# A four-layer block on one core: the second attention's queries and keys brought to heads by DMA instead of by VectorE

## The chip, the core and the metric

The kernel runs on one core of one Trainium2 chip. The metric is device time in microseconds (us) of one execution. TensorE (PE) does the matmuls and the 128x128 turnings (a matmul with the identity), VectorE (DVE), ScalarE (ACT) and GpSimd (POOL) do the elementwise work, and SyncE (SP) issues nearly all DMAs. Everything is float32; the first feed-forward layer uses float32r pieces. In PSUM there are eight banks of 128x512 float32.

## The reference

Four layers follow each other on x of (8, 512, 256), each ending in `x = layernorm(x + layer(x))`: a retention layer, a feed-forward layer with ternary weights, the second attention, and a mixture of eight experts. The change is in the third, whose heart is this (H = 16 heads of HD = 16 features):

```python
xn = _rms(x, g1)
Q, K, V = (einsum('bsf,ef->bse', xn, W).reshape(b, s, H, HD) for W in (Wq, Wk, Wv))
pQ, pK = elu(Q), elu(K)
Q1, Q2 = split(pQ, 2, axis=-1);  K1, K2 = split(pK, 2, axis=-1)
kv1 = einsum('bshe,bshd->bsed', K1, V) * SCALE     # sums over the heads of one token
kv2 = einsum('bshe,bshd->bsed', K2, V) * SCALE
w1  = einsum('bshe,bsed->bshd', Q1, kv1)
w2  = einsum('bshe,bsed->bshd', Q2, kv2)
attn = w1 - lmb * w2
```

After it come two RMS norms, a two-matmul GELU layer and the residual. The attention is over the 16 heads of one token, not over tokens.

## The kernel before

**Tiling.** The kernel works on one batch element b (512 tokens, four chunks c of 128) at a time. A group of 8 tokens with 16 heads makes 128 rows, so the attention of 8 tokens is one 128x128 score matrix in which `tokmask` keeps the pairs of equal tokens. A chunk has 16 such groups. The queries and keys of a group must lie with the 16 features of a head on 16 partitions; four groups r sit on partitions 32r to 32r+15 of one tile, and their four score matmuls (16 rows each) run beside each other on PE.

**Stages.** Each batch runs through stages a0, a1, a2 (retention), b and bn (feed-forward and norm), c1 (second attention), c2 (its norms, GELU layer and residual, store to DRAM), t (choice of experts). When four batches of a group are through, r (route) and then g, d, h, e, s (gather, experts, combine) run for the group. w loads expert weights (1 MB each).

**c1 before.** `transposed` turns the 512 tokens to x2T (features on partitions) through PE and ACT. `project(c)` makes q and k of a chunk as tokens x 512 features (line 1400) and v (line 1406); ACT and DVE apply ELU with the token's RMS factor as a scale and write `pad`; two DVE stream transposes (32x32 blocks; `V.transpose`) turn `pad` into `hT`, one for q and k and one for v. `scores(c)` turns the v part back with four PE transposes to `v_tp` (line 1454), which ACT copies to `vt`, and makes the scores `hs` (16 groups, line 1460). `masked` moves scores to `hm` with the mask (three of four on DVE, one on ACT and POOL). `values(c)` multiplies `vt` with them into `at_ps` (line 1475), and one DVE stream transpose moves that to `ap`. All of it stays on the chip.

**Order.** All engines' instruction orders are fixed at build time. A planner, `interleave`, walks through the streams of stages; each op has a cost in us and is placed on its engine's time line, and each PE step waits (`need`) until its input and a PSUM bank are free by the plan. Of the steps that can go next, it takes the smallest `t + w * due`, where `due` comes from a table `turns` in the source, one number for each stage; before, w is 0.0, so `due` only breaks ties. When PE would idle over 1.4 us by the plan, it places filler matmuls (`spare`, line 337) to keep PE's clock up. SP's DMAs are placed in the order of their planned times; SP's own issue time is not in the plan. Every engine, SP included, runs its list in order, so an instruction that waits holds back all behind it.

**DMA in flight.** A DMA issued by SP waits for the eighth DMA before it (the program gives them eight semaphores in turn), so at most eight are under way.

**Buffers.** Named slots with counts, such as `ex` (3 tiles of 128x512), `T` (3), `b8` (2), and the banks of PSUM; a stage takes slots when it begins or when it needs them, and the plan's free times order the reuse.

Of the kernel before, what the change touches and what calls it, by code (L numbers as in the profile page):

```python
# [46 lines left out]
def _constants():  # L47
# [15 lines left out]
        "parity": np.stack([hp % 2 == 0, hp % 2 == 1], 1),  # L63
        "tokmask": (i[:, None] % 8 == i[None, :] % 8) * QK_SCALE,
# [17 lines left out]
def tile_layers(ctx: ExitStack, tc: tile.TileContext, ins, out, at):  # L82
# [31 lines left out]
    iota, tokid = table("iota"), table("tokid")  # L114
# [7 lines left out]
    y_d = [dram.tile([TG + P, D], F32, name=f"y_d{g}") for g in range(G)]  # L122

# [19 lines left out]
    NVZ, XH = 3, 2  # L143
    SCM = 8
    XB, TB, EX, B8 = 4, 3, 3, 2
    EW = 3

    class Plan:
# [13 lines left out]
                hT3=2, ln=2, vz=NVZ, xh=XH,  # L162
# [129 lines left out]

    def later(t):

        return "other", t

    def interleave(streams, due):
# [11 lines left out]
        first = {"a0", "a1", "b", "c1", "h", "e", "s", "d", "z"}  # L309
        while any(queues):  # L310
            best = None
            for i, q in enumerate(queues):
# [15 lines left out]
                choice = t + 0.0 * due(key), due(key), i, on_pe, t  # L328
# [58 lines left out]
    def transposed(dst, src, t, cost=0.44):  # L387

        for k in range(NK):
            yield from need(t)  # L390
            ps = bank("tp")
            for c in range(NC):
                T.transpose(ps[:, c * P : (c + 1) * P], src[:, c, k * P : (k + 1) * P], ident)
            done = op(ACT, 0.59, pe(cost), A.copy, dst[:, k, :], ps, bank=ps)
        return done
# [222 lines left out]
    with ExitStack() as stages:  # L618
# [224 lines left out]
        pad = [wts.tile([P, 3 * D + HD], F32, name=f"pad_{i}") for i in range(2)]  # L843

        def by_head(pd, i, n):

            return pd[:, i * D : (i + n) * D].rearrange("p (h d) -> p h d", d=HD)

        def blocks(pd, i, n):

            v = by_head(pd, i, n)
            (pstep, pn), (hstep, hn), (dstep, _) = v.ap
            return bass.AP(v.tensor, v.offset, [(pstep, pn), (hstep, hn), (dstep, 2 * HD)])


        def prepare_l1():
            for i in range(2):
                op(POOL, 0.1, Plan.t, GP.memset, pad[i][:, 3 * D :], 0.0)
# [32 lines left out]
            def lam():  # L891
                nc.vector.tensor_tensor(lamv, le[:, 1:2], le[:, 0:1], ALU.subtract)
                return nc.vector.tensor_scalar(lamv, lamv, LAMBDA_INIT, None, ALU.subtract)

            op(DVE, 0.3, t, lam)
# [469 lines left out]
        def stage_bn(b):  # L1365
# [5 lines left out]
            rs1 = wk.tile([P, 2, NC], F32, tag="rms1", bufs=2, name=f"rms1_{b}")  # L1371

            def squares():
                nc.vector.tensor_tensor(rs1[:, 0], rs, rs, ALU.mult)
                return nc.vector.tensor_tensor(rs1[:, 0], rs1[:, 0], mv[:, :, 1], ALU.mult)
# [3 lines left out]
            t = rsqrt(rs1[:, 0], rs1[:, 0], 1.0, RMS_EPS, t)  # L1379
            t = op(DVS, 0.17, t, V.tensor_scalar, rs1[:, 1], rs1[:, 0], -1.0, None, ALU.mult)  # L1380
# [4 lines left out]

        def stage_c1(b):
            x2, rs1, scaled = x2s[b]
            x2T = slot_tile(wk, "T", [P, NK, S], f"x2T_{b}")
            ready = yield from transposed(x2T, x2, 0.0)
            ap = slot_tile(wk, "b8", [P, NC, H, 32], f"ap_{b}")  # L1390
            hTs = {}

            def project(c):

                cs = slice(c * P, (c + 1) * P)
                pd = pad[c % 2]
                yield from need(ready, n=2)
                qk = bank("qk_ps")
                for k in range(NK):
                    T.matmul(  # L1400
                        qk, x2T[:, k, cs], l1T[:, k, 0:2, :].rearrange("p a d -> p (a d)"),
                        start=(k == 0), stop=(k == NK - 1),
                    )
                v = bank("v_ps")
                for k in range(NK):
                    T.matmul(
                        v[:, :D], x2T[:, k, cs], l1T[:, k, 2, :], start=(k == 0), stop=(k == NK - 1)
                    )
                t = pe(2.4)
                t_qk = max(t - 0.8, scaled)  # L1410
                t = max(t, scaled)

                rs, rsn = rs1[:, 0, c : c + 1], rs1[:, 1, c : c + 1]
                ex = slot_tile(wk, "ex", [P, S], "ex")
                pqk = by_head(pd, 0, 2)
                e1 = op(ACT, 0.68, t_qk, A.activation, ex, qk, AF.Relu, scale=rsn, use=ex)
                e2 = op(
                    ACT, 0.68, t_qk, A.activation,
                    pqk, qk.rearrange("p (h d) -> p h d", d=HD), AF.Relu, scale=rs,
                )  # L1420
                release(qk, max(e1, e2))
                e1 = op(EXP, 0.63, e1, A.activation, ex, ex, AF.Exp, scale=-1.0)
                ev = op(
                    ACT, 0.46, t, A.activation, by_head(pd, 2, 1),
                    v[:, :D].rearrange("p (h d) -> p h d", d=HD), AF.Copy, scale=rs, bank=v,
                )
                t = op(
                    DVS, 0.69, max(e1, e2), V.scalar_tensor_tensor, pqk,
                    ex.rearrange("p (h d) -> p h d", d=HD), -1.0, pqk, ALU.add, ALU.add, drop=ex,
                )  # L1430
                q2 = by_head(pd, 0, 1)[:, :, HD // 2 :]
                t = op(ACT, 0.35, t, A.activation, q2, q2, AF.Copy, scale=lamv)


                hT = slot_tile(wk, "hT3", [P, 4, 3 * P], f"hT_{b}_{c}")
                turned = hT.rearrange("p g (x t) -> p x g t", t=8)
                ev = op(
                    DVE, 0.7, ev, V.transpose, turned[:, 2 * H :],
                    blocks(pd, 2, 1), use=hT,
                )  # L1440
                t = op(
                    DVE, 1.22, t, V.transpose, turned[:, : 2 * H],
                    blocks(pd, 0, 2),
                )
                hTs[c] = hT
                return max(t, ev)

            def scores(c, t):

                hT = hTs[c]  # L1450
                yield from need_scores(t, 5)
                ps = bank("v_tp")
                for g in range(4):
                    T.transpose(ps[:, g * P : (g + 1) * P], hT[:, g, 2 * P :], ident)
                vt = wk.tile([P, 4, P], F32, tag="vt", bufs=2, name=f"vt_{b}_{c}")
                sc = [bank(f"hs_{b}_{c}_{r}") for r in range(4)]
                for g in range(4):
                    for r in range(4):
                        rows = slice(32 * r, 32 * r + HD)
                        T.matmul(  # L1460
                            sc[r][:, g * P : (g + 1) * P], hT[rows, g, P : 2 * P], hT[rows, g, :P],
                            start=True, stop=True,
                        )
                t = pe(1.69)
                give(hT, t)
                scm, done = masked(f"hm_{b}_{c}", sc, tokmask, t)
                e = op(ACT, 0.59, t - 1.1, A.copy, vt.rearrange("p g n -> p (g n)"), ps, bank=ps)
                return vt, scm, max(done, e)

            def values(c, vt, scm, t):  # L1470
                yield from need(t)
                acc = bank("at_ps")
                for g in range(4):
                    for r in range(4):
                        T.matmul(
                            acc[32 * r : 32 * r + 32, g * P : (g + 1) * P],
                            vt[:, g, 32 * r : 32 * r + 32], scm[r][:, g, :], start=True, stop=True,
                        )
# [8 lines left out]
            turned = []  # L1487
            for c in range(2):
                turned.append((yield from project(c)))
            for c in range(NC):  # L1490
                full = yield from scores(c, turned[c])
                if c + 2 < NC:
                    turned.append((yield from project(c + 2)))
                    if c + 2 == NC - 1:
                        give(x2T, Plan.now)
                done = yield from values(c, *full)
            aps[b] = ap, done
# [408 lines left out]
        def after(*keys):  # L1906
# [24 lines left out]
            "c2": [(("c2", b), after(("c1", b)), {"m4": 2}, stage_c2(b)) for b in range(B)],  # L1931
            "bn": [(("bn", b), after(("b", b)), {}, stage_bn(b)) for b in range(B)],
            "c1": [
                (("c1", b), after(("bn", b), ("p", 1)), {"b8": 1, "T": 1}, stage_c1(b))
                for b in range(B)
            ],
# [55 lines left out]
                -0.67, 7.77, 120.34, 10.79, 107.15, 110.57, 2.87, 102.1, -5.72, 13.07, 11.66, -10.22,  # L1992
                100.38, 2.06, 1.79, 103.04
            ],
            "p": [-7.83, -1.63],
            "a0": [
                16.46, -2.45, 101.53, 13.47, 112.66, 108.34, 4.55, 2.62, 5.58, 13.37, 7.99, 9.62, 106.9,
                15.6, 13.84, 112.95
# [69 lines left out]
```

## Time and profile before

| what | value |
|---|---|
| median of 3 runs | 912.31 us (911.98 to 914.94) |
| the profiled execution's own time | 912.14 us |
| its span, first to last instruction | 910.1 us |
| busy PE, DVE, ACT, POOL | 857.3, 644.4, 567.3, 367.1 us |
| granted PE clock, mean over the span | 0.981 |
| DMA packets | 54252, 64.97 MB |

PE "busy" is the union of matmul records whose ends are modelled, so that a matmul's record is longer than the step from its start to the next one's. Where a price of PE time is wanted, the distance of starts in the timeline is the better measure. A float32 matmul is two records. The list of waits names for each wait the thing that came last.

### The profile page before, as it was taken

What the parts mean: (1) busy time and instruction counts of PE and PEld (TensorE: products, weight loads), DVE (VectorE), ACT (ScalarE), POOL (GpSimd) and SP (SyncE); (2) the same over time, 40 slices, a digit from 0 to 9 for tenths busy, and PEclk for the clock granted to TensorE, in tenths of its full rate; (3) what the DMA queues carried; (4) which work ended last, traced back from release to release, by engine and by line L of the source; (5) the groups of instructions that cost most, each with busy time, mean ns of one, the idle gap of its engine ahead of it and who ended that gap; (6) DMA issues with size and microseconds to landing.
All of it is one profiled execution on the core that took longest, in us unless ns stands there. A gap on an engine that the chain in (4) does not pass through costs nothing. (4 is left out here: it accounts for less than half of the span.)

```text
span 910.1 us, 20170 instructions
## 1 busy us (share of the span) xinstructions
PE 857.3 (94%) x8114; PEld 712.4 (78%) x8114; DVE 644.4 (71%) x1631; ACT 567.3 (62%) x1146; POOL 367.1 (40%) x379
## 2 busy tenths in 40 slices
PE   7989999999999999999999899998899999999942
PEld 5878978878788787878878678877577989899941
DVE  3944688888888989878778897988988643514123
ACT  2447587868779776876877867687767353132212
POOL 2124454535453533445524443353354222452233
PEclk9999999999999999999999999999999999999975
DMA  6120101010010020010200004101220557278743
GB/s 198 37 88 24 36 13 36 13 36 2 13 48 13 2 81 3 12 36 2 71 1 2 1 25 165 68 1 48 93 82 25 177 162 246 37 232 273 227 119 107
DMA packets 54252, 64.97 MB, mean 71 GB/s; under 512 B 5936, under 2 KB 49136, under 8 KB 54160
## 3 DMA queue, kind: packets, MB, share of 16 engines
q1 hardware_dynamic: 50304, 58.12, 19.0%
q0 software_dynamic: 3856, 5.57, 3.1%
q8 instruction: 64, 1.05, 0.5%
q14 instruction: 28, 0.23, 0.1%
HBM read 47.95 MB, written 15.73 MB: 70 GB/s over the span
## 5 line engine op out<-in xcount | busy, mean ns | idle before, releaser
L226 POOL TENSOR_TENSOR fsq<-fsq,fh 128x256 f32<-128x256 f32 x96 | 71.2, 742 | 61.1 <-ACT fh L226 43.4
L226 DVE SCALAR_TENSOR_TENSOR fT<-fh,lnf,fT 128x256 fp32r<-128x256 f32 x128 | 71.7, 608 | 21.5 <-ACT fT L226 21.3
L1710 PE MATMUL wo_ps<-e_hT,wo 128*128 128x160 f32 x512 | 74.1, 301 | 0.0
L1683 PE MATMUL wi_ps<-xsT,wi 128*128 128x160 f32 x512 | 73.9, 300 | 0.0
L226 DVE TENSOR_TENSOR scm<-sc,cst 128x512 f32<-128x512 f32 x96 | 61.2, 682 | 16.3 <-PE sc L1060 16.2
L1275 PE MATMUL fc_ps<-x1T,fcT 128*128 128x256 f32 x512 | 69.4, 288 | 2.7 <-ACT fh L226 1.9
L1683 PEld LDWEIGHTS wi_ps<-xsT,wi 128*128 128x128 f32 x512 | 70.6, 190 | 1.3 <-issue 1.1
L1316 PE MATMUL pr_ps<-prT,fT 128*128 128x258 f32 x512 | 69.8, 290 | 1.6 <-DVE hm L226 1.3
L1710 PEld LDWEIGHTS wo_ps<-e_hT,wo 128*128 128x128 f32 x512 | 70.3, 190 | 1.2 <-issue 0.6
L226 ACT ACTIVATE e_hT<-wi_ps 128x480 f32<-128x480 f32 (+1 forms) x48 | 25.0, 525 | 73.0 <-PE wi_ps L1683 73.0
L1275 PEld LDWEIGHTS fc_ps<-x1T,fcT 128*128 128x128 f32 x512 | 63.1, 189 | 7.3 <-ACT fh L226 2.3
L1316 PEld LDWEIGHTS pr_ps<-prT,fT 128*128 128x128 f32 x512 | 64.3, 189 | 4.0 <-DVE hm L226 1.7
L991 PE MATMUL qk_ps<-xT,wqkv 128*128 128x256 f32 x256 | 63.4, 399 | 4.0 <-ACT xT L226 2.7
L226 POOL TENSOR_TENSOR scm<-scm,cst 128x512 f32<-128x512 f32 x32 | 41.4, 1294 | 60.3 <-ACT scm L226 24.7
L226 DVE STREAM_TRANSPOSE hT<-pad 128x512 f32<-128x512 f32 (+1 forms) x64 | 60.1, 962 | 6.1 <-ACT pad L226 5.6
L226 POOL DMA_INDIRECT y_d<-eo,srci x21 | 32.8, 1563 | 73.9 <-ACT eo L226 20.7
L1400 PE MATMUL qk_ps<-l1T,x2T 128*128 128x512 f32 x128 | 61.3, 601 | 0.0
L226 DVE TENSOR_TENSOR hm<-hs,cst 128x512 f32<-128x512 f32 x96 | 60.7, 678 | 0.7 <-PE hs L1460 0.7
L226 POOL TENSOR_TENSOR ln<-ln,mhalf 128x4 f32<-128x4 f32 x32 | 33.7, 1054 | 67.7 <-DVE ln L226 67.5
L991 PEld LDWEIGHTS qk_ps<-xT,wqkv 128*128 128x128 f32 x256 | 49.1, 198 | 13.4 <-ACT xT L226 5.8
L226 ACT ACTIVATE fT<-fh,lnf 128x256 fp32r<-128x256 f32 x128 | 57.8, 498 | 1.2
L226 POOL TENSOR_TENSOR hm<-hm,cst 128x512 f32<-128x512 f32 x32 | 40.9, 1279 | 42.5 <-ACT hm L226 21.2
(267 smaller groups left out, 2057.5 us busy)
## 6 DMA issues: line engine op xcount, KB each, us to landing
wi<-in_L_ffn_wi SPq DMA_DIRECT2D x13, 1024.0 KB, 7.8
wo<-in_L_ffn_wo SPq DMA_DIRECT2D x13, 1024.0 KB, 7.7
xh<-in_L_attn_x SPq DMA_DIRECT2D x16, 256.0 KB, 2.7
x<-in_L_attn_x SPq DMA_DIRECT2D x8, 512.0 KB, 4.1
x_d<-a SPq DMA_DIRECT2D x8, 512.0 KB, 2.9
y_d<-a SPq DMA_DIRECT2D x8, 512.0 KB, 4.3
z<-y_d SPq DMA_DIRECT2D x8, 512.0 KB, 6.8
out<-z SPq DMA_DIRECT2D x8, 512.0 KB, 3.2
```

Source lines behind the costliest of these rows:

```text
L226: heapq.heappush(Plan.events, (t, Plan.count, shares, t + cost, lambda: fn(*args, **kw)))
L991: T.matmul(ps[:, m * HT : (m + 1) * HT], wqkv[:, k, which * D + m * P : which * D + (m + 1) * P], xT[:, k, :], start=(k == 0), stop=(k == ...
L1275: T.matmul(ps[:, j * HT : (j + 1) * HT], fcT[:, k, f * P : (f + 1) * P], x[:, k, :], start=(k == 0 and x is low), stop=(k == NK - 1 and x ...
L1316: T.matmul(acc[:, : D + 2], hs[:, part, f, c * P : (c + 1) * P], prT[:, f, :], start=(f == 0 and part == 1), stop=(f == NF - 1 and part == 0),
L1400: T.matmul(qk, x2T[:, k, cs], l1T[:, k, 0:2, :].rearrange("p a d -> p (a d)"), start=(k == 0), stop=(k == NK - 1),)
L1683: T.matmul(ps[:, f * CAP : (f + 1) * CAP], wi[:, k, (f3 + f) * P : (f3 + f + 1) * P], x[:, k, es], start=(k == 0), stop=(k == NK - 1),)
L1710: T.matmul(ps[:, m * CAP : (m + 1) * CAP], wo[:, f, m * P : (m + 1) * P], hT[:, f, :], start=(f == 0), stop=(f == NF - 1),)
```

## The change

- c1 now first scales the tokens by their RMS factor (`x2n`, four ACT ops), turns them to x2T with the token order inside each 16 tokens permuted, and projects q and k feature-major (128 features x 512 tokens, weights stationary); ELU is on these, the factor of the second half of q's features is one more ACT pass (`lamq`). k first, then q, then v in two halves.
- Each of the four 128x512 results is stored to DRAM (`qk_d`), and v in four DMAs (`v_d`).
- A new stage `hd` reads them back: for each chunk eight DMAs of 16 partitions x 32 x 16 (32 KB in runs of 64 bytes) into `hh`, and for each batch 16 DMAs of 8 partitions x 64 x 16 (32 KB in runs of 64 bytes) into `vt`. `hh` has three slots, `vt` two.
- A new stage `ca` holds scores and values. `scores` reads `hh` with a step of two elements; the PE turnings of v, their ACT copies and the DVE turnings of `pad` are gone. The DVE turning of `at_ps` to `ap` stays.
- `ex` has 5 slots (3), `vz` 2 (3); c1 takes two `T`; c1(b) waits for ca(b-2).
- The weight w is 0.001226 and all of `turns` is new, so the order of all stages is new.

The core of the diff (lines of after):

```diff
-    NVZ, XH = 3, 2
+    NVZ, XH = 2, 2
+    HH = 3
-    XB, TB, EX, B8 = 4, 3, 3, 2
+    XB, TB, EX, B8 = 4, 3, 5, 2
...
-                choice = t + 0.0 * due(key), due(key), i, on_pe, t
+                choice = t + 0.001226 * due(key), due(key), i, on_pe, t
...
         def stage_c1(b):
+            x2n = slot_tile(wk, "T", [P, NC, D], f"x2n_{b}")
+            for c in range(NC):
+                t = op(ACT, 0.49, max(Plan.t, scaled), A.activation, x2n[:, c, :], x2[:, c, :], AF.Copy,
+                    scale=rs1[:, c : c + 1], use=x2n if c == 0 else None)
+            ready = yield from transposed(
+                x2T.rearrange("p k (a t b) -> p k a b t", t=8, b=2), x2n, t,
+                lambda ps: ps.rearrange("p (a b t) -> p a b t", b=2, t=8))
+            for which in (1, 0):
+                for m in range(NK):
...
+                    e1 = op(ACT, 0.6, t, A.activation, ex, ps, AF.Relu, scale=-1.0, use=ex)
+                    e2 = op(ACT, 0.6, t, A.activation, qk, ps, AF.Relu, use=qk)
+                    e1 = op(EXP, 0.63, e1, A.activation, ex, ex, AF.Exp, scale=-1.0)
+                    t = op(DVS, 0.69, max(e1, e2), V.scalar_tensor_tensor, qk, ex, -1.0, qk, ALU.add, ALU.add, drop=ex)
+                    if which == 0:
+                        t = op(ACT, 0.63, t, A.activation, qk, qk, AF.Copy, scale=lamq)
+                    dma(t, qk_d[b % 2][which * D + m * P : which * D + (m + 1) * P, :], qk)
+                    ends.append(t + 2.5)
+            for half in range(2):
...
+                t = op(ACT, 0.6, pe(1.73), A.copy, v.rearrange("p c d -> p (c d)"), ps, use=v, bank=ps)
+                for i in range(2):
+                    dma(t + 0.4 * i, rows_v[2 * half : 2 * half + 2, i].rearrange("c p d -> p c d"), v[i::2])
+                ends.append(t + 2.5)
+
+        def stage_hd(b):
+            got = qk_d[b % 2].rearrange("(j d) (c r a u) -> c r a d j u", d=HD, r=4, a=2, u=16)
+            v = v_d[b % 2].rearrange("(g t) (h d) -> h t g d", t=8, d=HD)
+            for c in range(NC):
+                if c > 0:
+                    yield from hold_later("hh")
+                hh = slot_tile(wk, "hh", [P, 2, 2 * H, 16], f"hh_{b}_{c}")
+                for r in range(4):
+                    for a in range(2):
+                        dma(Plan.t + 0.8 * r + 0.4 * a, hh[32 * r : 32 * r + HD, a], got[c, r, a])
+                heads[b].append((hh, Plan.t + 7.0))
+                if c == 0:
+                    for h in range(H):
+                        dma(Plan.t + 3.2 + 0.4 * h, vt[8 * h : 8 * h + 8, ...], v[h])
+                    landed = Plan.t + 14.0
+            heads[b].append((vt, landed))
+
+        def stage_ca(b):
+            def scores(c):
+                hh, landed = heads[b][c]
+                yield from need_scores(landed, 4)
+                pair = hh.rearrange("p a j (h u) -> p a j (h u)", j=2)
...
-                            sc[r][:, g * P : (g + 1) * P], hT[rows, g, P : 2 * P], hT[rows, g, :P],
+                            sc[r][:, g * P : (g + 1) * P], pair[rows, g // 2, 1, g % 2 :: 2],
+                            pair[rows, g // 2, 0, g % 2 :: 2], start=True, stop=True,
...
+            def values(c, scm, t):
+                vt, landed = heads[b][NC]
+                yield from need(max(t, landed))
...
+            "hd": [(("hd", b), [("c1", b)], {"vt": 1, "hh": 1}, stage_hd(b)) for b in range(B)],
+            "ca": [(("ca", b), [("c1", b)], {"b8": 1}, stage_ca(b)) for b in range(B)],
```

## The prediction

> **What bounds the kernel now.** I read the page first, then busy time by stretches of the span, PE's waits, the groups by form, and short timelines.
>
> ```profile
> PE 857.3 (94%) x8114; PEld 712.4 (78%) x8114; DVE 644.4 (71%) x1631; ACT 567.3 (62%) x1146; POOL 367.1 (40%) x379
> ```
>
> That is the whole span of 910.1 us. The view of stretches has the stretch and its length, then busy PE, weight loads, DVE, ACT and POOL, the granted clock, DMA share and GB/s:
>
> ```profile
> 100.00:550.00 450.00, 442.60 (x4607) 358.54 (x4606) 374.72 (x894) 346.28 (x697) 202.62 (x212) 1.00 0.07 23
> 550.00:700.00 150.00, 142.90 (x1309) 112.05 (x1308) 128.37 (x334) 107.01 (x213) 63.31 (x68) 1.00 0.21 68
> ```
>
> The second attention runs inside these two. PE is busy 98% and 95% there, DVE 83% and 86%, ACT 77% and 71%, and DMA 7% and 21%. So PE is the bound, DVE the next, and DMA nearly free. PE's waits from 100 to 700 us confirm it: no wait on the block turnings stands in the list, and its longest lines are small.
>
> ```profile
> PE inv_ps L578 <- DVE route L226: 3.6, 5, 1.2
> PE fc_ps L1275 <- ACT fh L226: 1.9, 2, 1.3
> PE at_ps L1475 <- POOL hm L226: 1.5, 3, 0.9
> ```
>
> The whole list there comes to about 14 us. So taking work from DVE and ACT can win little by itself; taking work from PE wins that work; and a new wait in PE's list costs its full length.
>
> **What is removed and added.** The groups by form (busy us, mean ns):
>
> ```profile
> L226 DVE STREAM_TRANSPOSE hT<-pad 128x1024 f32<-128x1024 f32 x32 | 39.1, 1221 | 3.3 <-ACT pad L226 2.9
> ...
> L226 DVE STREAM_TRANSPOSE hT<-pad 128x512 f32<-128x512 f32 x32 | 22.5, 704 | 2.8 <-ACT pad L226 2.7
> ...
> L1454 PE MATMUL v_tp<-cst_ident,hT 128*128 128x128 f32 x128 | 20.7, 285 | 0.0
> ```
>
> DVE loses 39.1 + 22.5 = 62 us; its 32 ELU passes stay, as do the 22.6 us that turn `at_ps` to `ap`. ACT loses the four passes that write `ex` and `pad` (21.8 + 21.8 + 14.8 + 12.8) and the copies to `vt` (18.8), 90 us. It gets 64 passes of 128x512 at about 0.59 us, 32 for `x2n` at 0.5 to 0.59, 16 for `lamq` at 0.63 and 16 copies of v at 0.58, 75 us; the program order also has 27 table loads instead of 37, at 1283 ns each. ACT is 28 us lighter. None of this is on PE's path; by the list of waits it is worth 0 to 14 us, and I take 8, since the waits on `route` are not of this kind.
>
> PE loses the 128 turnings `v_tp`. Projections have the same columns as before. A row of starts gives their pitch:
>
> ```profile
> 321.34 0.66 PE L1454 MATMUL v_tp<-cst_ident,hT 128*128 128x128 f32 x4
> 321.93 1.17 PE L1460 MATMUL hs<-hT 16*128 16x128 f32 x32
> 323.03 1.98 PE L1400 MATMUL qk_ps<-l1T,x2T 128*128 128x512 f32 x4
> ```
>
> Four turnings take 0.59 us from start to start, 32 x 0.59 = 18.9 us; without a step between they take 0.47 (starts 289.76 and 290.23 of another four), 15 us. I take 17. The program of after has 77 filler matmuls where before has 89; at 0.43 us of pitch that is 5 us, since fillers are executed whether PE needs them or not. The score matmuls read with a step of two elements, which no row shows; a chunk's 32 records take 1.10 us (above). If they stayed the same: 0. If the step halved their rate: +1.1 x 32 = 35 us. The nearest row is the copy into `vz` in runs of 16 among gaps, 581 ns against 579 for a whole 128x512, so I take 0 and keep part of the upper end in the range.
>
> **The DMA path, and who waits.** SP gets 56 new DMAs for each batch: 448 more on top of 112. PE's order in after is fixed, so I asked how much PE work stands between the end of v's projection of batch b and its first scores, the cover for the way through DRAM. For batch 2 there stand 8 fillers (8 x 0.43), 10 turnings (x 0.12), one set of 8 retention scores (8 x 0.15), a set of `r_ps` and state matmuls (2.5): 8.1 us. For the eight batches: 9.0, 19.7, 8.1, 19.0, 8.2, 31.6, 10.6, 16.0 us. What has to be covered is: the copy of v (0.58), two v stores and, because the DMAs of chunks 0, 1 and 2 are queued in turn, 22 of the 24 first reads, all one after the other on SP, and then a landing. SP's rate is in its timeline:
>
> ```profile
> 44.95 0.46 SPq L226 DMA_DIRECT2D x_d<-zrow  x1
> 45.45 0.46 SPq L226 DMA_DIRECT2D y_d<-zrow  x1
> ```
>
> ```profile
> 9.50 0.38 SPq L753 DMA_DIRECT2D lnwb<-in_L_ffn_ln_w  x1
> 10.25 0.38 SPq L753 DMA_DIRECT2D lnwb<-in_L_ffn_ln_b  x1
> ```
>
> From 44.10 to 47.56 seven issues follow at 0.49 us. The page's and the DMA view's landings are 1.8 us for the `router` load (256 packets of 32 bytes) and 2.7 for the 256 KB of `xh`. 24 x 0.49 + 0.58 + 1.8 to 2.7 = 14.1 to 15.0 us; I take 14.5. Covers fall short by 5.5, 6.4, 6.3 and 3.9 us in batches 0, 2, 4, 6: 22 us of PE standing still. The plan's own figure (2.5 for the store, 7.0 for the chunk) has no issue time of SP in it, which is why it put the scores there.
>
> The far end is a rate of 0.75 us, the distance of the two `lnwb` issues, the only ones with as many short pieces (1024 each). Then the need is 20.6 us, and the shortfalls are 11.6, 0.9, 12.5, 1.6, 12.4, 0, 10.0, 4.6: 54 us. The engines' own time for short packets is no bound:
>
> ```profile
> DMA packets 2182, 0.23 MB, mean 117 GB/s; under 512 B 2072, under 2 KB 2072, under 8 KB 2182
> ...
> q1 hardware_dynamic: 2182, 0.23, 88.4%
> ```
>
> From 12.5 to 14.5 us, 2182 packets took 88.4% of 16 engines: 13 ns each at most, so 512 of them 0.42 us over 16 engines, below SP's 0.49. [...]
>
> A stall of over 3 us also costs clock. Around 343 us a few short gaps in PE and its weight loads were enough (seventh column, the clock):
>
> ```profile
> 343.00:344.00 1.00, 0.65 (x10) 0.40 (x14) 0.97 (x4) 0.80 (x3) 0.61 (x1) 0.79 0.09 16
> 344.00:345.00 1.00, 1.00 (x28) 0.89 (x24) 0.93 (x5) 0.53 (x2) 0.00 (x0) 0.50 0.00 0
> ```
>
> About 3.4 us ran at half speed, 1.7 us lost; four stalls make 7 us. Then `vt`: its 16 reads follow the 24, so it is there after 0.58 + 42 x 0.49 + 2 = 23 us. Covers from v's end to the first values are 20.2, 44.8, 16.7, 27.6, 17.9, 36.0, 16.9 and 21.9 us, to which the first stall adds its length; batches 2 to 4 then just suffice, and batch 6 falls short by 2. There SP also has two 1 MB expert loads between `vt`'s reads, 2.1 MB at the 281 GB/s that the view of stretches has from 800 to 850 us, 7 us. I take 8 us for batch 6, with 0 and 15 as ends. Chunk 3's reads have covers of 35 us and more: 0. What else is queued behind SP's reads (the next x and expert loads, the stores of c2) is wanted tens of us later: 0, but up to 2 us a batch, 16 us, if one waits at SP's head for a late c2. The four `x2n` passes put 2 us before c1's turnings, where PE has other batches' work in its list: 0, or up to 2 us a batch without it.
>
> **Sum.** Against the profiled execution, 912.14 us (its span and 2.0 around it; the median, 912.31, is the same to 0.02%): -17 -5 -8 +22 +7 +8 = +7, so about 919 us. The end is not changed: the last expert matmuls and the tail are in both programs.
>
> **Rivals.** (a) The cover holds: the stages drift apart in the run, as PE's list is never as fast as planned, and the reads land in time. Then -17 -5 and -8 to -14 for the lighter DVE and ACT: 876 to 890, say 882 us. For it speak the idle DMA (0.07) and that half of the batches have cover enough; against it the 14.5 us. It decides where the first reads land within 10 us of v's end. (b) SP or the reads are slow, 0.75 us each: 54 for the scores, 29 for `vt` (need 34 us against the covers with their first stall), 12 for the clock, -30: 977 us. (c) The turning is not what it says: DVE keeps the `ap` turnings and no one waited for the others, so only PE's 17 + 5 count and the stalls are half as long (11 + 4 + 4): about 909 us, no change.
>
> **How the numbers follow.** Forecast 0.47, (a) 0.32, (b) 0.13, (c) 0.08. The forecast's own range is 903 to 935 (ends of landing, batch 6 and SP's head). Ends of the overall range: 880, which leaves out the lower half of (a)'s gain beyond 882, and 972, which leaves out most of (b) above its figure: about 2 in 10. What a measurement can tell from no change is 0.3%, 2.7 us. Faster: 0.30 of (a), 0.03 of (c), 0.04 of the forecast, 0.37. Same: 0.07. Slower: 0.56.
>
> **What would show it.** Right, if PE's waits after list `hs` on a DMA `hh` in batches 0, 2, 4 and 6 with 3 to 7 us each, SP's issues come 0.45 to 0.55 us apart, and the clock drops there. Wrong, if there are no such waits (a); if `hh` reads land over 5 us after issue (b); or if score records take over 1.5 us a chunk. If PE's busy time falls by less than 20 us while no wait grows, the removed turnings were hidden.

## The result: 8.7% slower

The changed kernel took 994.75 us (median of 4 runs, 987.73 to 996.70), the kernel before 913.62 beside it: a ratio of 1.087 (1.081 to 1.093). The forecast of 919 had the direction right, the place in part and the size wrong: the time is beyond the upper end of 972. The profiled execution took 993.45 us, its span 991.7.

The busy line of the page, the two stretches of the second attention, and PE's waits (us in total, times, longest), all of the kernel after:

```profile
PE 866.7 (87%) x7962; PEld 720.5 (73%) x7962; DVE 585.8 (59%) x1560; ACT 540.1 (54%) x1104; POOL 358.4 (36%) x378
```

```profile
100.00:550.00 450.00, 413.51 (x4117) 336.48 (x4116) 306.71 (x795) 299.51 (x617) 181.55 (x196) 0.95 0.33 53
550.00:700.00 150.00, 120.24 (x1106) 95.26 (x1106) 100.80 (x260) 89.70 (x173) 53.79 (x61) 0.88 0.68 100
```

```profile
PE at_ps L1514 <- DMA hh<-qk_d: 50.6, 6, 17.7
PE hs L1497 <- DMA hh<-qk_d: 31.8, 15, 4.6
PE inv_ps L589 <- DVE route L231: 2.5, 1, 2.5
```

DVE and ACT are lighter, as they should be (585.8 and 540.1 us against 644.4 and 567.3). PE is not busier in what it has to do; it stands, 82.4 us of it for `hh` and `vt`, and its granted clock in the two stretches fell from 1.00 to 0.95 and 0.88. The wait of the values is booked on `hh` because the two kinds of reads share the eight semaphores; the values read `vt`, and in the run below without `vt` reads no wait of `at_ps` on a DMA is left.

SP in batch 0, and PE beside it (start, length, instruction):

```profile
155.09 4.58 SPq L231 DMA_DIRECT2D v_d<-v  x4
159.84 12.56 SPq L231 DMA_DIRECT2D hh<-qk_d  x21
...
172.98 2.06 SPq L231 DMA_DIRECT2D hh<-qk_d  x3
175.08 6.99 SPq L231 DMA_DIRECT2D vt<-v_d  x8
```

```profile
167.15 0.51 PE L1497 MATMUL hs<-hh 16*128 16x128 f32 x4
170.12 0.47 PE L1497 MATMUL hs<-hh 16*128 16x128 f32 x2 [2.46 <-DMA hh<-qk_d]
173.16 1.24 PE L1497 MATMUL hs<-hh 16*128 16x128 f32 x16 [2.57 <-DMA hh<-qk_d]
178.62 1.22 PE L1497 MATMUL hs<-hh 16*128 16x128 f32 x10 [4.23 <-DMA hh<-qk_d]
```

In these rows SP issues an `hh` read every 0.53 to 0.6 us and a `vt` read every 0.8 to 0.9. The first scores begin at 167.15, and each group of matmuls waits for the next read: 9.3 us in three stands. The bracket is the idle time before the row, and its releaser.

Where did the 81.6 us between the spans (910.1 and 991.7) come from? I cut each span into slices of 1 us and added up PE's busy time and granted clock. Of the matmul records, 67.1 us lie in slices at half clock, 3.3 before; a step of a matmul takes twice as long there (fillers start 427 ns apart, outside 216), so half of such a record is lost. So at full clock PE's records would be 866.7 - 33.5 = 833.2 us, before 857.3 - 1.7 = 855.6: 22.4 us less. PE's idle time grew from 52.8 to 125.0, by 72.2. And half clock took 31.9 more. -22.4 + 72.2 + 31.9 = 81.7. The removed work is a gain of just the size worked out; waiting and clock cost 104.

### The profile page after: what moved, and what is told of

It reads as the page before. It is cut to its first block, busy times and chain, and to the rows that moved or that the text cites. A ratio compares the mean times of both kernels' runs of the same rounds, so it can differ in the third digit from the quotient of the medians.

```text
span 991.7 us, 20412 instructions
## 1 busy us (share of the span) xinstructions
PE 866.7 (87%) x7962; PEld 720.5 (73%) x7962; DVE 585.8 (59%) x1560; ACT 540.1 (54%) x1104; POOL 358.4 (36%) x378
## 3 DMA queue, kind: packets, MB, share of 16 engines
q8 instruction: 63, 1.03, 0.5%
## 5 line engine op out<-in xcount | busy, mean ns | idle before, releaser
L1514 PE MATMUL at_ps<-hm,vt 128*32 128x128 f32 x1024 | 40.4, 302 | 51.7 <-DMA hh<-qk_d 50.6
L1497 PE MATMUL hs<-hh 16*128 16x128 f32 x1024 | 53.8, 325 | 32.7 <-DMA hh<-qk_d 31.8
L1497 PEld LDWEIGHTS hs<-hh 16*128 16x128 f32 x1024 | 43.4, 219 | 45.5 <-issue 22.7
L231 DVE SCALAR_TENSOR_TENSOR fT<-fh,lnf,fT 128x256 fp32r<-128x256 f32 x128 | 61.3, 524 | 25.3 <-ACT fT L231 25.0
L1320 PE MATMUL pr_ps<-prT,fT 128*128 128x258 f32 x512 | 74.5, 301 | 0.0
L1279 PE MATMUL fc_ps<-x1T,fcT 128*128 128x256 f32 x512 | 73.4, 303 | 0.6 <-DVE x1T L231 0.4
L1514 PEld LDWEIGHTS at_ps<-hm,vt 128*32 128x32 f32 x1024 | 30.4, 120 | 59.0 <-issue 55.4
L1728 PEld LDWEIGHTS wi_ps<-xsT,wi 128*128 128x128 f32 x512 | 72.2, 194 | 0.6 <-issue 0.2
L1279 PEld LDWEIGHTS fc_ps<-x1T,fcT 128*128 128x128 f32 x512 | 68.5, 207 | 4.4 <-issue 1.7
L231 DVE TENSOR_TENSOR scm<-sc,cst 128x512 f32<-128x512 f32 x96 | 61.0, 683 | 16.7 <-PE sc L1064 16.7
L231 ACT COPY hm<-hs 128x512 f32<-128x512 f32 x32 | 18.6, 580 | 88.1 <-PE hs L1497 88.1
L231 POOL TENSOR_TENSOR hm<-hm,cst 128x512 f32<-128x512 f32 x32 | 35.6, 1114 | 85.5 <-ACT hm L231 44.2
```

What stands on the lines that cost most here:

```text
L231: heapq.heappush(Plan.events, (t, Plan.count, shares, t + cost, lambda: fn(*args, **kw)))
L1279: T.matmul(ps[:, j * HT : (j + 1) * HT], fcT[:, k, f * P : (f + 1) * P], x[:, k, :], start=(k == 0 and x is low), stop=(k == NK - 1 and x ...
L1320: T.matmul(acc[:, : D + 2], hs[:, part, f, c * P : (c + 1) * P], prT[:, f, :], start=(f == 0 and part == 1), stop=(f == NF - 1 and part == 0),
L1497: T.matmul(sc[r][:, g * P : (g + 1) * P], pair[rows, g // 2, 1, g % 2 :: 2], pair[rows, g // 2, 0, g % 2 :: 2], start=True, stop=True,)
L1514: T.matmul(acc[32 * r : 32 * r + 32, g * P : (g + 1) * P], vt[:, at_ : at_ + 2 * HD], scm[r][:, g, :], start=True, stop=True,)
L1728: T.matmul(ps[:, f * CAP : (f + 1) * CAP], wi[:, k, (f3 + f) * P : (f3 + f + 1) * P], x[:, k, es], start=(k == 0), stop=(k == NK - 1),)
```

## The experiments

Theory 1: PE stands in its written order for late `hh` and `vt`, and runs at half clock after it. Rivals: the new stage order itself; traffic on the DMA engines; and, found on the way, reads that hold other transfers up in SP's list (theory 3). Times are medians; the kernel before ran beside them at 911.9 to 912.9. "Idle" is PE's from 60 us to 40 us before the end, "half" the matmul records at half clock, both from slices of 1 us (before: 17.8 and 3.3 us; after: 95.6 and 67.1).

### No reads, reads unused, one kind of read

```diff
-  hh = slot_tile(wk, "hh", ...); for r ...: for a ...: dma(..., hh[...], got[c, r, a])
-  for h in range(H): dma(..., vt[8 * h : 8 * h + 8, ...], v[h])
-  pair = hh.rearrange("p a (j h) u -> p a j (h u)", j=2)
+  pair = cst[:, : 4 * P * 2].rearrange("p (a j v) -> p a j v", a=2, j=2)
```

The run with unused reads keeps the DMAs and lets both matmuls read `cst`; the other two leave out one kind.

> The changed kernel without the 48 reads a batch of stage hd (32 hh, 16 vt); the six DRAM stores of q, k and v a batch and the whole order stay. Scores multiply the constant table and values a constant vt, and the attention's share in the residual sum is scaled to about a thousandth so that the routing stays even; so the second attention is not computed. Theory 1 (TensorE stands in its written order for late hh and vt, and runs at half clock after each stand): both go, and what is left is the gain of the forecast's own terms, 912 - 17 - 5 - 8 = 882; expected 875 to 895. Rival 1 (the new stage order is itself worse, whatever lands when): 950 or more, near the 995 of the changed kernel. Rival 2 (traffic on the DMA engines slows everything else): 875 to 895 too, told apart by the next run.

> All 48 reads a batch are issued as in the changed kernel, but scores and values multiply the constant table, so no matmul waits for a read; the attention's share is scaled down as in the run without reads. Theory 1: within 6 us of the run without reads, 875 to 900. Rival 2 (the reads' packets hold up the stores, expert loads and gathers): most of the 110 us is still there, 950 or more. Between the two, the excess over the run without reads is what the traffic costs.

> The 16 vt reads a batch are left out and vt holds a constant; the 32 hh reads stay and the scores use them (share scaled down as before). Theory 1: the hh waits stay (32 of 82 us of visible waits) and with them their part of the half clock: about 885 + 110 x 32/82 = 928, range 915 to 945; the hh waits of TensorE stay near 30 us. Rival (the vt reads cost nothing by themselves, only the hh reads in front of them are late): 970 or more.

> The 32 hh reads a batch are left out and the scores multiply the constant table; the 16 vt reads stay and the values use them (share scaled down as before). Theory 1 with waits that add: 885 + 110 x 51/82 = 953. Theory 1 with one queue: the vt reads now are first in SP's list, 24 x 0.55 = 13 us earlier, so that their need falls from about 30 to 17 us and most covers hold: 885 to 905. If vt is slow by its own reads (16 x 0.85 us and a landing) and not by what stands ahead of it: 920 or more.

| run | us | ratio (interval) | idle | half |
|---|---|---|---|---|
| no reads | 887.5 | 0.974 (0.970 to 0.978) | 16.7 | 6.6 |
| reads unused | 920.6 | 1.009 (1.006 to 1.012) | 46.8 | 22.8 |
| no vt reads | 923.8 | 1.013 (1.011 to 1.015) | 39.2 | 36.5 |
| no hh reads | 907.8 | 0.994 (0.991 to 0.997) | 31.5 | 27.6 |

None of the four computes the second attention; its share in the residual is scaled to about a thousandth. With the same PE order and no reads, the change wins 25 us: the order is good, and the whole loss of 107 us comes in with the reads. The first rival falls. By itself each kind of read costs less than its share (36 and 20 us, where 82 us of waits had promised 41 and 66): `vt` is late in the changed kernel to a large part because 24 `hh` reads stand ahead of it in SP's list. Without them the values still stand 11.8 us and the time is 907.8, just above the 885 to 905 expected for one queue and far below the 953 for waits that add.

The run with unused reads is a miss of theory 1. No matmul waits for a read there, and yet 33 us are lost. Its waits of PE, and of ACT:

```profile
PE inv_ps L589 <- DVE route L231: 19.8, 3, 16.2
PE pr_ps L1320 <- DVE fT L231: 13.0, 1, 13.0
```

```profile
ACT fh L231 <- DMA qk_d<-qk: 14.0, 1, 14.0
```

ACT stood 14.0 us for a `qk_d` store of c1, since that store gives back an `ex` tile; DVE stood behind ACT, and PE 13.0 us behind DVE. Where the store was, SP's timeline shows:

```profile
499.69 13.87 SPq L231 DMA_DIRECT2D hh<-qk_d  x24
513.60 12.68 SPq L231 DMA_DIRECT2D vt<-v_d  x15
526.32 0.71 SPq L231 DMA_DIRECT2D hh<-qk_d  x1
527.08 0.58 SPq L231 DMA_DIRECT2D vt<-v_d  x1
527.70 3.88 SPq L231 DMA_DIRECT2D hh<-qk_d  x7
531.67 0.90 SPq L231 DMA_DIRECT2D qk_d<-qk  x2
```

Behind all 48 reads of the batch, 32 us of SP's list. The planner stamps the reads 0.4 us apart, all three chunks at the same time, so a store that comes due 10 us after the first read is written behind all of them. The 16.2 us on `route` are of the same kind: DVE stood 15.7 us for a `y_d<-a` store, which SP issued at 655.41 behind 36 reads and two 1 MB loads.

### Stores behind reads, or traffic?

```diff
-  dma(Plan.t + 0.8 * r + 0.4 * a, hh[...], got[c, r, a])
+  dma(Plan.t + lag + 1.10 * r + 0.55 * a, hh[...], got[c, r, a])   # chunk 0, vt, chunks 1 and 2
-  Plan.t + 3.2 + 0.4 * h,
+  Plan.t + 4.40 + 0.85 * h,
```

Both runs keep all 48 reads unused and the lists of all other engines; the second has 0.8 and 1.2 us.

> As the run with unused reads (scores and values multiply the constant table, share scaled down), the same 48 reads a batch and the same order on TensorE, ScalarE, VectorE and GpSimd; only SP's list differs: the reads are stamped at the pace that the trace shows (0.55 us an hh, 0.85 us a vt: chunk 0, then vt, then chunks 1 and 2), so that stores and loads that come due meanwhile stand between them, and not behind all of them. In the run with unused reads TensorE lost 13.0 us to fT and 16.2 us to route, behind DVE's 14.0 and 15.7 us, while SP issued 41 reads in a row from 504.6 to 531.6 us and a qk_d store after them. Theory 3 (reads hold other transfers in SP's list): 887 to 900. Theory 2 (the packets themselves hold up other transfers on the DMA engines): 913 to 925, as before.

> As the run with unused and reordered reads, with the reads stamped 0.8 us (hh) and 1.2 us (vt) apart, so that still fewer stand ahead of a store that comes due; the other engines' lists are the same, the bytes and runs too (scores and values multiply the constant table, share scaled down). Stores behind reads in SP's list: 887 to 896. Traffic on the DMA engines: 900 or more, as before.

Measured: 903.3 (0.990, 0.987 to 0.992) and 898.3 (0.984, 0.982 to 0.987). The same bytes, 22 us less. What is left against 887.5 has again the form of a store behind reads: in the second run ACT stands once for a `qk_d` store, and PE behind it.

```profile
PE hs L1498 <- ACT qk L231: 6.5, 1, 6.5
```

That stand and the half clock (20.8 us against 6.6, so 7 us lost) cover the remaining 11 us. Both times lie between their two expectations all the same, so traffic may cost a little. Of the 33 us, 17 went with the new places in SP's list, at about the pace that the reads had before; 5 more went with reads further apart, which thins the traffic as well. In the changed kernel this term is hidden behind the longer waits for the reads themselves.

### The order of the reads, and their form

```diff
-  dma(Plan.t + 0.8 * r + 0.4 * a, hh[...], got[c, r, a])
+  dma(Plan.t + 1.6 * (c in (1, 2)) + 0.4 * r + 0.2 * a, hh[...], got[c, r, a])
```

> The changed kernel with one order changed: SP issues the eight hh reads of chunk 0 first and those of chunks 1 and 2 after them, instead of all three in turn; every other engine's list is the same, and so are the vt reads' places. The first scores then need some 8 x 0.55 + 4 = 8 to 9 us in place of 14 to 18, against covers of 8.1 to 31.6. Theory 1: the hh waits of TensorE fall from 31.8 to 10 to 18 us, the vt waits stay near 50; with about 0.6 us of half clock per us of wait, 965 to 985. If the reads stand on the DMA engines and not in SP's list: 990 to 998.

Measured 998.3 (1.094, 1.091 to 1.097). A miss, and a useful one: the time is the rival's, but its sign, scores that still wait, is absent. PE's waits:

```profile
PE at_ps L1514 <- DMA hh<-qk_d: 67.1, 4, 24.2
PE at_ps L1514 <- DMA vt<-v_d: 31.6, 2, 20.1
```

No wait of `hs` on a DMA is left in the list, 31.8 before, and the values wait 98.7 us instead of 50.6. PE's order has the scores, a few other steps and then the values; whoever comes sooner to the values waits there. The end is set by the last `vt` read, and that is 40 issues away however the first 24 are turned.

Then the form of the reads, one kind at a time, with PE's order unchanged. `vt` by token:

```diff
-  for h in range(H):  dma(..., vt[8 * h : 8 * h + 8, ...], v[h])      # 512 runs to 8 partitions
+  for tk in range(8): dma(..., vt[tk::8, ...], v[tk])                 # 1024 runs to 16 partitions
```

`hh` in runs of 128 bytes (the tokens of a group lie four apart):

```diff
-  hh = slot_tile(wk, "hh", [P, 2, 2 * H, 16], ...)   # 8 reads for each chunk
+  hh = slot_tile(wk, "hh", [P, 2 * H, 32], ...)      # 4 reads for each chunk
-  sc[r][...], pair[rows, g // 2, 1, g % 2 :: 2], pair[rows, g // 2, 0, g % 2 :: 2]
+  sc[r][...], pair[rows, 1, g::4], pair[rows, 0, g::4]
```

> The changed kernel with one form changed: vt comes in 8 reads a batch, one for each token of eight, of 1024 runs of 64 bytes to 16 partitions eight apart, instead of 16 reads, one for each head, of 512 runs to 8 partitions. Bytes and runs are the same, and so is the order on every other engine. If a vt read is slow because it writes only 8 partitions (16 hh reads of the same 512 runs go out every 0.53 us, a vt read every 0.85 us), a batch's vt takes 8 x 1.06 = 8.5 us or less instead of 13.6: the waits on vt fall from 51 to about 25 us and with their half clock the time to 945 to 970. If a run costs the same wherever it lands, 8 x 1.7 us: 985 to 1000.

> The changed kernel with tokens of a score block four apart instead of two, so that an hh read takes 32 tokens in runs of 128 bytes: 16 hh reads a batch of 512 packets instead of 32, half of hh's packets; v is stored in 8 parts a batch instead of 4. The order on TensorE is the same. Theory 1: 12 issues instead of 24 ahead of the first scores and of vt: need of the first scores 12 x 0.55 + 4 = 11 us, of vt some 6 us less; waits fall from 82 to about 45 us, time 940 to 965. If an hh read of 128-byte runs takes twice as long to issue or land, nothing is won: 985 to 1000.

By token: 951.5 (1.042, 1.036 to 1.048), 43 us won by the form of one read. The waits are 20.6 us on `at_ps` and 22.0 on `hs`. Batch 2 on SP in this run, and in the changed kernel:

```profile
366.29 12.82 SPq L231 DMA_DIRECT2D hh<-qk_d  x24
379.15 8.45 SPq L231 DMA_DIRECT2D vt<-v_d  x8
```

```profile
368.78 12.70 SPq L231 DMA_DIRECT2D hh<-qk_d  x24
381.53 12.80 SPq L231 DMA_DIRECT2D vt<-v_d  x15
```

The same 8192 runs take 8.5 us instead of 13.6 (16 reads): at the pace of such a row a run costs 1.03 ns in both the `hh` reads (0.53 us for 512) and these (1.06 for 1024), and 1.66 where a read goes to only 8 partitions. It is the pace of a row, not SP's price of one issue: in the changed kernel's batch 2 the first four `vt` reads took SP 0.39 to 0.48 us each, the nine after them 0.80 to 1.00. SP is held once a few such reads are under way; by what, no view names.

Among the packets of 64 bytes the changed kernel's trace has some of 4: 348 for 21.9 `hh` reads (370 to 381.5 us) and 81 for 10.3 `vt` reads (384 to 394 us), that is about 16 and 8 for each read, as many as it has partitions. What they are, and on which engines a read ran, the records don't say.

In the changed kernel from 172 to 186 us, when batch 0's `vt` was read, the mean busy share of the DMA engines was 90% (the column before the last); during batch 2's `hh` reads, from 369 to 381.5 us, it was 65%:

```profile
172.00:186.00 14.00, 8.61 (x48) 7.38 (x49) 3.47 (x7) 2.62 (x5) 2.92 (x4) 0.52 0.90 90
```

Wide runs: 1007.0 (1.104, 1.097 to 1.110). 12 reads take 6.8 to 6.9 us instead of 12.7, so SP gains 6 us a batch, and the `hs` wait falls from 31.8 to 14.7. But the `vt` reads behind them take longer (15 in 16.5 us), the wait of the values stays at 51.4, and the score matmuls pay for their step of four elements. Records of `hs` (min, median, max in ns), in the changed kernel and in this one:

```profile
L1497 PE MATMUL hs<-hh x1024: 269/275/579, 167.1 to 801.2; 16*128 16x128 f32 x171
```

```profile
L1496 PE MATMUL hs<-hh x1024: 403/411/599, 166.9 to 812.3; 16*128 16x128 f32 x171
```

A step of two costs 5 ns of 270, a step of four 141. A chunk's 32 records took 1.10 us from start to start in the kernel before, 1.16 with a step of two and 2.19 with a step of four: 33 us for 32 chunks (27 by the busy time of the group, 80.9 against 53.8, of which more was at half clock in the changed kernel). That is enough to turn the gain into a loss.

### An order that knows the landings

The wide reads again, now with the reads stamped one after the other and honest landings, so that the planner puts other work or fillers in front of scores and values:

```diff
-  heads[b].append((hh, Plan.t + 7.0))
+  heads[b].append((hh, Plan.t + lag + 6.70))
-  landed = Plan.t + 14.0
+  landed = Plan.t + 20.30
```

> As the run before (runs of 128 bytes), and in the list of due times the reads are stamped one after the other (0.55 us an hh, 0.85 us a vt; chunk 0, vt, then chunks 1 and 2) with landings 4.5 us after the last stamp (first scores 6.7 us, vt 20.3 us, chunk 1 22.5 us after the stage begins) where the changed kernel has 7.0 and 14.0; TensorE's order follows these numbers and puts other work there. Theory 1 and 3 (waits come from landings that the written order does not know, and from stores behind reads): waits on hh and vt under 20 us in all, 895 to 925. If the order can't fill the time, or the transfers stay as late: 950 or more.

Measured 1008.6 (1.104, 1.101 to 1.107), a miss: the waits on `hh` and `vt` fell to 22.7 us, and the time did not. The wide score matmuls are one part. The fillers are another: their records doubled.

```profile
L348 PE MATMUL spare<-cst,cst_ident 128*128 128x256 f32 x308 | 73.7, 392 | 1.4 <-ACT fh L231 0.9 <-ACT qk L231 0.6
```

154 such records took 39.1 us in the changed kernel. With its turns there is not enough other work at these places, and the wait is filled, not used. How much an order depends on the stages it was made for, the kernel before shows with the changed kernel's turns and weight:

> The kernel before with only the order changed: the turns and the weight of the due times (0.001226) of the changed kernel. Nothing of the second attention's path is changed. If the new order is a part of the 25 us that the changed kernel without reads gains: 885 to 905. If the gain is the work removed (17 us of turnings, 5 us of filler matmuls): 912 or more, since these turns were made for other stages; 912 to 940.

Measured 976.8 (1.070, 1.063 to 1.076), beyond both expectations, with 472 filler records against 178. So the turns have to be made anew for every set of landings, and the next three runs do that: they rearrange the turns until the plan's own end is early.

> The whole second attention, with three edits to the changed kernel: vt in 8 reads a batch, one for each token of eight; the reads stamped at the pace of the traces, chunk 0, then vt, then chunks 1 and 2 (0.53 us an hh read, 1.06 us a vt read), with landings 4.0 us after the last stamp (first scores 8.2 us, vt 16.7, chunk 1 20.9, chunk 2 25.2 after the stage begins); and the turns of the stages rearranged so that the plan's own end is early with these numbers: 873.7 us. The plan of the changed kernel ends at 866.5 with landings that don't hold, and its run without reads had a span of 884.8, 18 us more. Theory 1 and 3 (the loss is waiting for landings that the plan did not know, and stores behind reads): 873.7 + 18 + 2 = 894, range 886 to 910, waits on hh and vt under 10 us in all. If reads through DRAM cost TensorE's time however they are ordered: over 925.

> As the run before, but stage c1 projects v first and issues the 8 vt reads itself while q and k are still projected, so that after c1 only the hh reads are left (landings 8.2, 12.5 and 16.7 us after the stage hd begins for chunks 0, 1, 2); turns rearranged for it, the plan's own end 875.8. Theory 1 and 3: 875.8 + 18 + 2 = 896, range 886 to 912. A rival for this one: the vt reads now stand ahead of the q and k stores in SP's list and hold them up, so ScalarE's ex and qk tiles come free late: 915 or more, with waits of ACT on qk_d.

> As the run with v first, the whole computation, with later landings in the plan: hh reads 5.0 us after their last stamp, at 0.55 us each (chunk 0 9.4 us after the stage hd begins, then 13.8 and 18.2), vt 5.0 us after its last, q and k stores 4.5 us instead of 2.5; turns rearranged for these, the plan's own end 883.5. The order then has fewer stands and more filler or later stages. If the loss is an order written with landings that don't hold: no hh or vt waits over 2 us, half clock under 10 us, 883.5 + 18 = 901, range 894 to 908, faster than the kernel before. If the path through DRAM costs TensorE's time beyond its waits: 910 or more again.

| run | us | ratio (interval) | waits on hh, vt | idle | half |
|---|---|---|---|---|---|
| vt by token, order anew | 941.6 | 1.032 (1.029 to 1.034) | 28.3 | 53.2 | 48.5 |
| v first, order anew | 912.9 | 1.000 (0.998 to 1.003) | 5.6 | 30.2 | 24.3 |
| v first, later landings | 918.8 | 1.007 (1.006 to 1.008) | 0.5 | 36.9 | 18.9 |

The first is in the range of its rival (over 925). It still missed its landings: by the plan `vt` is there 16.7 us after the stage's begin, and in batch 0 SP issued its last `vt` read 20.7 us after the first `hh` read (160.37 and 181.00). With v projected first, `vt` is read while q and k are still being projected; this run is 29 us faster, at the time of the kernel before and just above its range, though its turns differ too. Its rival, reads that hold up the stores of q and k, shows in one place: ACT stood 7.5 us for a `qk_d` store, until 532.86. The last run has next to no wait on a read left and is not faster; it is in the range of its rival (910 or more). It does not return the block's values throughout, for a reason that stays open, so it is read for its time alone. Its longest wait is in the experts' tail, where the kernel before has one of 11.6 us too:

```profile
PE eo_tp L1792 <- DVE eoT L231: 13.0, 3, 12.0
```

So 912.9 is the best that was reached with the path through DRAM, no faster than before. They are 25 and 31 us above the run without reads. In the first, PE idles 13.5 us more, 5.6 of it for reads, and half clock costs 9 more; in the second 20.2 more, 0.5 of it for reads, and 6. So honest landings removed the waits for the reads, and did not bring the time expected of that. Whether other turns would win the rest back, or the reads cost it, stays open.

## Why the prediction was wrong in size

**PE's removed work (-17, -5): right.** 22.4 us, counted at full clock. **Relief of DVE and ACT (-8): not shown in this size.** The run without reads wins 25.3 us of span: 21.0 of matmul records, 5.9 of idle, less 1.6 of clock. Of the 5.9 only 1.1 lie between 60 us and 40 us before the end (17.8 against 16.7), where the second attention runs.

**First scores (+22): right place, a third too small.** PE stood in batches 0, 2, 4 and 6 as named, for 9.3, 4.8, 9.0 and 8.1 us where 5.5, 6.4, 6.3 and 3.9 were worked out; with two small ones, 31.8. The need of 14.5 us was short: from the end of v's last projection (155.84 + 1.89) to the last `hs` group that waited, at 178.62 in batch 0, it was 20.9, and 15.7, 20.9 and 21.9 in batches 2, 4 and 6. The v stores took 0.6 us each instead of 0.49, the reads 0.53 to 0.6, and the landing of the last read that counts took 2.5 us from its issue in batch 2 and 4.7 to 5.6 in the others, instead of 1.8 to 2.7. In batch 0 a 512 KB `x` load had gone out just before; whether that is why, no run shows.

**vt (+8): the step that failed.** It was given SP's 0.49 us a read and a 2 us landing, 23 us in all, and priced at 8 us for batch 6 alone; it measured 50.6. The first values of batch 2 began at 399.80, and v's last projection ended at 364.84 + 1.89: 33.1 us; batches 3, 4 and 7 needed 37.7 to 38.9, batch 6 needed 48. Against covers of 17 to 28 us, batches 2, 3, 4, 6 and 7 stood 7.3, 6.0, 5.6, 17.7 and 13.6 us: 50.6 in all, with a wait of 0.5 in batch 0. In batch 2 the 33.1 us were 2.1 to the first read (1.6 worked out), 12.7 for the 24 `hh` reads (11.8), 14.3 for the 16 `vt` reads (7.8) and 4.0 after them (2.0). The largest part is the pace of the `vt` reads, 0.85 us and not 0.49. The text had the row for it, 13 ns a packet, and called the engines no bound because it spread 512 packets over 16 of them. An estimate from that row and the measured 0.85 us: some 8 engines at work (512 x 13 ns / 0.85 us = 7.8); over how many a read is spread, no run shows. Batch 7 was left out besides: its cover of 21.9 us was short of 23 by the text's own numbers. The reason given for batch 6 was right: two 1 MB expert loads between its reads.

```profile
681.72 7.09 SPq L231 DMA_DIRECT2D vt<-v_d  x7
688.91 1.10 SPq L231 DMA_DIRECT2D wi<-in_L_ffn_wi  x1
690.12 0.40 SPq L231 DMA_DIRECT2D wo<-in_L_ffn_wo  x1
690.57 9.73 SPq L231 DMA_DIRECT2D vt<-v_d  x5
```

**Clock (+7): too small by more than a factor of four.** The text took one dip of 3.4 us for each of four stalls, from the only one before the tail; the changed kernel lost 31.9 us more than the one before. Each of its ten stands of over 3 us (3.58 to 17.71) had half clock in it, from 2.4 to 5.1 us after the stand's begin where it was not on already. Two of the stretches of the changed kernel (length, busy time of five engines, clock):

```profile
677.00:691.00 14.00, 8.15 (x65) 6.20 (x66) 4.36 (x15) 2.88 (x7) 2.06 (x2) 0.51 1.18 39
697.00:714.00 17.00, 2.94 (x52) 2.59 (x56) 4.78 (x9) 0.00 (x0) 0.00 (x0) 0.52 0.75 116
```

Half clock lasts 10 to 17 us in seven stretches, stands included: 13.7 us in three where short stands follow each other, 10.2 in two after a single stand of 6.0 and 7.3 us, and 17.1 in two with a stand of 13.6 and 17.7. In all it is 113 us in eleven stretches before the tail, with 67.1 us of matmul records in them.

The eleven stretches lasted 3.41, 6.83, 10.24, 13.65 or 17.07 us. Work alone did not end one at once: after the stand of 6.0 us PE was busy in 3.40 of 3.40 us from 503.0 to 506.4, and the clock was still 0.50 until 509.8. So one dip of 3.4 us for each stall is the least. What sets the length, no run here tests.

**SP's head (0, up to 16): short.** Where nothing hides them, reads that no one waits for cost 33 us, at least 17 of them by stores that stand behind reads. The bound counted only a read waiting at SP's head, not 32 us of reads ahead of a store that gives back a tile.

**The score step of two (0, up to 35): right.** It costs 0.05 us a chunk, 1.7 in all; a step of four costs 33.

**The rivals.** (a), a cover that holds, fell. (b) came nearest: 54 + 29 = 83 us of waits against 82.4, and with the measured 31.9 for the clock instead of 12 it gives 997. That the sum fits is luck: (b) had 54 for the scores and 29 for `vt`, measured were 31.8 and 50.6, and its one pace of 0.75 us lies between the 0.53 of the `hh` reads and the 0.85 of the `vt` reads. It had 0.13 because the 0.75 us stood on a single pair of issues.

## What to carry to other kernels

Where an engine's order is fixed at build time, a new transfer is as good as the landing time that the order was made with: count all issues ahead of it on its queue, at a pace for its own form, and include the stores that will stand behind it. Take the pace from a row with the same runs and the same number of partitions, or carry both ends into the forecast itself. And where PE will stand, price the stand with its half clock: here 32 us on top of 72.

## What was not expected of the hardware

- In a row of such reads SP issued one of 512 runs of 64 bytes every 0.53 us to 16 partitions and every 0.85 us to 8 (changed kernel, batch 2); one of 1024 runs to 16 partitions every 1.06; one of 512 runs of 128 bytes every 0.57. The first few reads to 8 partitions took 0.27 to 0.70 us.
- A matmul of 16x128 f32 took 270 ns with contiguous operands, 275 with a step of two elements, 411 with a step of four.
- Around a single stand of 6.0 us half clock lasted 10.2 us, 6.8 of them with PE busy throughout; the only stretch of the kernel before ahead of its tail, after short gaps, had 3.4 us.
